# A graph-attention layer on one core: POOL's gathers wait for the landing of the gather five in front, in place of a pace set by its own instructions

## The chip, the cores and the metric

The kernel runs on one core of a Trainium2 chip. The metric is the time of one execution in microseconds (us), measured on the device. PE is the tensor engine, DVE the vector engine, ACT the scalar engine, POOL the GpSimd engine, SP the sync engine, which issues most of the DMAs.

## The reference

The layer takes 12500 nodes of 128 numbers, 412500 edges sorted by their target, and 64 numbers for each edge. With layer norm and ReLU ahead, and the input added at the end, it computes for four heads of 32:

```python
h = (relu(layernorm(x)) @ W_node.T).reshape(12500, 4, 32)
e = (edge_attr_64 @ W_edge.T).reshape(412500, 4, 32)
att = sum(concat([h[src], h[dst], e], -1) * a, -1)
att = where(att > 0, att, 0.2 * att)
m = maximum(segment_max(att, dst), 0.0)
ex = exp(att - m[dst])
denom = segment_sum(ex, dst) + (412500 - deg)[:, None] * exp(-m)
out = x + segment_sum((ex / denom[dst])[:, :, None] * h[src], dst)
```

`h[src]` is the gather: a row of h for each of the 412500 edges.

## The kernel before

Edges are cut into 461 chunks of 896 (7 tiles of 128 edges), and 7 chunks make a batch: 66 batches, the last one with 6 chunks. A batch's rows lie in `hs`, 49 tiles of 128 rows by 144 numbers (h and two attention terms for each head, 576 bytes a row). There are four such buffers in a ring (`RING`), and batch b uses buffer b modulo 4.

Lead-in (lines 241 to 601): the 98 tiles of nodes are normed, multiplied with the weights and written to `table` in DRAM. The first 58 tiles of edges don't wait for the table: POOL gathers their raw rows of x (`gather_raw`, line 256) into the first two buffers, and they go through the same norm and product as the nodes, in groups of up to nine tiles. Raw tiles 0 to 48 are batch 0, raw tiles 49 to 57 are the first nine of batch 1. `lead_in` puts the steps of DVE, ACT and PE in an order that follows from a list of costs. DVE measures each raw tile (line 361) as it lands.

Main loop (from line 1120 on), written out by hand: in iteration b POOL gathers batch b + 1 out of `table`, one indirect DMA for each tile (`gather`, line 707), behind a small memset that waits for PE's last product with the batch that had the buffer. SP loads edge features (`eft`, line 643), the near logits of the targets (`lw`, line 651), `pen` and indices. DVE waits for batch b's rows (`weigh`, through `landed`, line 726), adds up logits (line 808), takes maxima by scans, and multiplies the rows with the weights (line 896); PE sums the rows by target (line 901); DVE adds what is summed to the accumulators (line 995). The last batch is done in two parts: `first_part` takes the tiles with t below `EARLY` (23 gathers), `second_part` the other 15.

How gathers and their readers are tied: each gather of a batch adds 16 to the batch's semaphore when it has landed, one of eight taken in turn by batches (`row_sems`), and the late tiles of the last batch have one of their own; DVE waits for the batch's whole count. The raw gathers have semaphores of the framework, eight in turn, and each waits for the one eight in front. The gathers of line 707 add 1 to `pace` when POOL has finished the instruction, and every second one waits until all but the newest instruction in front of it are finished:

```python
if paced[0] >= BEHIND and paced[0] % STEP == 0:
    nc.gpsimd.wait_ge(pace, paced[0] - BEHIND + 1)
```

Of the kernel before, what the change touches and what calls it, by code (L numbers as in the profile page):

```python
# [20 lines left out]
D = 128  # L21
# [10 lines left out]
CB = 2 * SB - 1  # L32
NBT = -(-NCH // CB)
# [9 lines left out]
EARLY = 4  # L43
# [3 lines left out]
XB = 9  # L47
LOOSE = 1
XS = 3
RAW = (T * CB, XB)  # L50
# [10 lines left out]
ROWSEMS = 8  # L61
# [1 line left out]
LEVELS = 5  # L63
RINGS = 8192
EPS = 1e-5
BEHIND = 2
STEP = 2
WQ = 50
COUNTED = 24
FIRST = 2  # L70
# [57 lines left out]
def kernel(  # L128
# [12 lines left out]
    nc = tc.nc  # L141
# [5 lines left out]
    table = padded[:NB * P, :]  # L147
# [74 lines left out]

    near_sems = [tc.alloc_semaphore(f"near{k}") for k in range(2)]
    near_done = [0, 0]
    late_sems, late_done = [tc.alloc_semaphore("late")], [0]
    pen_sems = [tc.alloc_semaphore(f"pen{k}") for k in range(2)]
    pen_done = [0, 0]
    row_sems = [tc.alloc_semaphore(f"rows{k}") for k in range(ROWSEMS)]
    row_done = [0] * ROWSEMS
    pace, paced = tc.alloc_semaphore("pace"), [0]  # L230

    indices = ctx.enter_context(tc.tile_pool(name="indices", bufs=AHEAD))

# [3 lines left out]
    def index(b):  # L237
        t = indices.tile([P, CB, 2, T], I32, name="ends")
        nc.sync.dma_start(t.rearrange("p q w t -> p (q w t)"), ends[:, chunk_of(b) * 2 * T:(chunk_of(b) + CB) * 2 * T])
        return t  # L240


    with (
        tc.manual_schedule(),
# [6 lines left out]
        early = [index(0)]  # L251
        raw = [pool.tile([P, T * CB, ROW], F32, name="hs") for pool in (opening, second)]

        def gather_raw(k):
            for i in range(RAW[k]):
                nc.gpsimd.indirect_dma_start(
                    out=raw[k][:, i, :D], out_offset=None, in_=x[:, :],
                    in_offset=bass.IndirectOffsetOnAxis(ap=early[k][:, i % CB, 0, i // CB:i // CB + 1], axis=0))

        gather_raw(0)  # L260

        wn = p1.tile([P, D], F32, name="wn")
# [63 lines left out]
        def load_rows(b0, n):  # L326

            s = Rows()
            s.b0, s.n, s.rows = b0, n, None
            at = b0 - NB  # L330
            if at >= 0:
                s.rows = raw[0][:, at:at + n, :] if at < RAW[0] else raw[1][:, at - RAW[0]:at - RAW[0] + n, :]
                s.x = s.rows[:, :, :D]
                return parted(s)
            full = min(n, (N - b0 * P) // P)
            s.x = p3.tile([P, XB, D], F32, name="xg", bufs=5)
            nc.sync.dma_start(s.x[:, :full, :],
                              x[b0 * P:(b0 + full) * P, :].rearrange("(b p) d -> p b d", p=P))
            if full < n:
                nc.vector.memset(s.x[:, full, :], 0.0)  # L340
                rest = N - (b0 + full) * P
                nc.sync.dma_start(s.x[:rest, full, :], x[(b0 + full) * P:N, :])
            return parted(s)

        def parted(s):

            n = s.n
            s.stats = p2.tile([P, XB, 2, 3], F32, name="stats", bufs=5)
            s.units = []
            for i0 in range(0, n, XS):  # L350
                u = Rows()
                u.s, u.i0, u.m = s, i0, min(XS, n - i0)
                u.hn = u.hT = None
                s.units.append(u)
            return s
# [342 lines left out]
    def gather(s, behind=None):  # L698

        if behind is not None:  # L700
            hold = nc.gpsimd.memset(gate, 0.0)
            tc.add_manual_dep(hold.ins, behind.ins.name,
                              mybir.DependencyInfo(mybir.DependencyClass.Sync, mybir.DependencyReason.DATA))
        for t, q in s.tiles:
            if paced[0] >= BEHIND and paced[0] % STEP == 0:
                nc.gpsimd.wait_ge(pace, paced[0] - BEHIND + 1)
            load = nc.gpsimd.indirect_dma_start(  # L707
                out=s.hs[:, t * CB + q, :], out_offset=None, in_=table[:, :],
                in_offset=bass.IndirectOffsetOnAxis(ap=s.ends[:, q, 0, t:t + 1], axis=0),
                engine_sem=pace)  # L710
            paced[0] += 1
            if s.b == NBT - 1 and t >= EARLY:
                by_itself(load, "late", late_sems, late_done, 0)
            else:
                by_itself(load, f"rows{s.b}", row_sems, row_done, s.b % ROWSEMS)

    def by_itself(load, group, sems, done, k):

        load.then_inc(sems[k], 16)
        done[k] += 16  # L720
        tc.add_to_no_dep_group(group, load.ins)
        tc.no_tile_sem_insts.add(load.ins.name)

    def landed(engine, group, sems, done, k, *what):

        wait = engine.wait_ge(sems[k], done[k], synchronizes=[engine.lower_ap(w) for w in what])  # L726
        if what:
            tc.declare_no_dep(wait.ins, group=group, reason="the semaphore counts these loads")
        tc.declare_fence(wait.ins, group=group)
        return wait.ins  # L730

    def load_pen(s):
        s.pen = pen_sb[:, s.b % 2, :]
# [46 lines left out]
    def weigh(s):  # L780

        last = EARLY * CB if s.b == NBT - 1 else T * CB
        s.fence = landed(nc.vector, f"rows{s.b}", row_sems, row_done, s.b % ROWSEMS,
               s.hs[:, RAW[1] if s.b == 1 else 0:last, :],
               *([s.ends[:, :, :, :]] if s.b < NBT - 1 else [])) if s.b else None
        open_weights(s)
        if s.b < NBT - 1:
            landed(nc.vector, f"pen{s.b}", pen_sems, pen_done, s.b % 2, s.pen)
        weigh_part(s, 0, EARLY if s.b == NBT - 1 else T)

    def open_weights(s):
# [45 lines left out]
    def sum_part(s, t0, t1):  # L837

        pa = open_sums()
        got = pa[:, :s.chunks * AW].rearrange("p (q d) -> p d q", d=AW)  # L840
        held = [min(tiles_of(s.c0 + q), t1) for q in range(s.chunks)]
        for q in range(s.chunks):
            if held[q] <= t0:
                nc.vector.memset(got[:, :, q], 0.0)
        for q in range(s.chunks):
            if held[q] > t0:
                multiply(s, q, t0, held[q])
                add_up(s, pa, q, t0, held[q])
        return got
# [11 lines left out]
    def second_part(s):  # L861

        places = columns(s.c0, s.chunks)
        landed(nc.vector, "late", late_sems, late_done, 0, s.hs[:, EARLY * CB:, :], s.ends[:, :, :, :])
        open_weights(s)
        weigh_part(s, *spans[1])
        r = work.tile([P, AW * (MC + 1)], F32, name="r")
        r = r[:, :AW * (len(spans) * s.chunks + 1)].rearrange("p (d c) -> p d c", d=AW)
        nc.scalar.copy(r[:, :, 1::len(spans)], s.first)
        got = sum_part(s, *spans[1])  # L870
        wrap_up(s.b - 1)
        nc.scalar.copy(r[:, :, 2::len(spans)], got)
        return r, s.breaks, places
# [63 lines left out]
    def columns(c, k):  # L937

        _, got = nc.values_load_multi_w_load_instructions(  # L939
            q_rel[0:1, c:c + k], engines=[ENG.DVE], min_val=0, max_val=WQ - 2,  # L940
            skip_runtime_bounds_check_because="near_columns keeps them from 0 to WQ - 2")
        return got
# [129 lines left out]
    def batch(b):  # L1072
        if b not in batches:
            s = batches[b] = Batch()
            s.b = b
            s.hs = None
            s.c0 = chunk_of(b)
            s.chunks = chunk_of(b + 1) - s.c0
        return batches[b]
# [15 lines left out]
    def wrap_up(last):  # L1095

        for b0, n, behind in parts():
            if behind == last:
                at = 4 * b0 - base_of(last)
                stores.append(finish(work, em_ps, b0, n, acc[:, at:at + 4 * n, :]))  # L1100
        if last < NBT - 1 and base_of(last + 1) > base_of(last):
            shift_sums((base_of(last + 1) - base_of(last)) // 4, base_of(last + 1) // 4,
                       nc.gpsimd if last == NBT - 2 else nc.vector)

    with tc.manual_schedule():
# [4 lines left out]
        for k in range(2):  # L1110
            clear_rows(batch(k))
            gather(batch(k))
# [8 lines left out]
        for b in range(NBT - 1):  # L1121
            s = batch(b)
# [11 lines left out]
            if b:  # L1134
                gather(batch(b + 1), scattered.get(b + 1 - RING))
# [46 lines left out]
        s = batch(NBT - 1)  # L1182
# [292 lines left out]
```

## Time and profile before

| | |
|---|---|
| three runs | 4073.79, 4075.94, 4077.2 us |
| profiled execution, its own time | 4069.02 us |
| its span, first to last instruction | 4067.2 us |
| mean granted clock of PE | 0.666 |
| busy: PE, DVE, ACT, POOL | 1392.1, 2428.0, 672.9, 3060.3 us |
| gathers: raw, out of the table | 58, 3165 |
| gathers' queue | 103136 packets, 237.36 MB |

The profile is of one execution. [...] "Idle before" is the time in which the engine did nothing ahead of an instruction, with what ended it. The name `POOL hs L707 <- DMA hs<-table,ends` is a gather that waited, by the trace, for an earlier one. In the timeline the columns are start, duration, engine, line, operation.

### The profile page before, as it was taken

To read this page: it belongs to the slowest core of one execution; us is meant where nothing else is said; L and a number is where in the kernel's file an instruction comes from. 1 tells how busy PE (TensorE), PEld (TensorE's weight loads), DVE (VectorE), ACT (ScalarE), POOL (GpSimd) and SP (SyncE) were. 2 spreads that over 40 slices of the span, in tenths; PEclk is the share of its full clock that TensorE was granted. 3 is DMA by queue.
4 is the path that set the end of the run, shared out by engine and by line. 5 is a ranking of instruction groups with operands and counts; after the bars stand their busy time and mean duration, and the time that the engine had idled before them with its cause. 6 is when DMAs were issued, how large, how long until landed. Compare 5 with 4: busy or idle time off the path is not lost. (4 is left out here: it accounts for less than half of the span.)

```text
span 4067.2 us, 19121 instructions
## 1 busy us (share of the span) xinstructions
PE 1392.1 (34%) x3549; PEld 560.2 (14%) x3549; DVE 2428.0 (60%) x3760; ACT 672.9 (17%) x1688; POOL 3060.3 (75%) x3295
## 2 busy tenths in 40 slices
PE   7453232233332332332332342332331332332331
PEld 5121011011111111110110110110110110110111
DVE  8786555556555567465566465566465465465576
ACT  8121011011011011011011011011011011011121
POOL 7777777777777777777777777777777777777775
PEclk9676666666665676675666665666665666666665
DMA  7543333333333333333333333333333333333332
GB/s 190 166 116 100 109 103 89 106 103 80 112 102 89 107 107 84 102 103 89 107 104 87 103 92 99 107 99 92 103 94 101 103 90 101 102 95 101 107 90 50
DMA packets 243658, 414.96 MB, mean 102 GB/s; under 512 B 71494, under 2 KB 155930, under 8 KB 243532
## 3 DMA queue, kind: packets, MB, share of 16 engines
q0 software_dynamic: 103136, 237.36, 24.4%
q1 hardware_dynamic: 127052, 168.97, 13.2%
q10 hardware_dynamic: 13344, 7.36, 0.6%
q14 instruction: 97, 0.79, 0.1%
q8 instruction: 29, 0.48, 0.1%
HBM read 397.91 MB, written 15.53 MB: 102 GB/s over the span
## 5 line engine op out<-in xcount | busy, mean ns | idle before, releaser
L707 POOL DMA_INDIRECT hs<-table,ends x3165 | 2996.3, 947 | 957.6 <-DMA hs<-table,ends 481.5
L901 PE MATMUL pa<-hs,hot 128*128 128x504 f32 x1820 | 931.6, 677 | 2541.7 <-ACT r L924 2460.7
L808 DVE TENSOR_TENSOR logits<-hs,pick 128x196 f32<-128x196 f32 x65 | 32.4, 499 | 1394.4 <-DVEq L726 1394.2
L901 PEld LDWEIGHTS pa<-hs,hot 128*128 128x128 f32 x1820 | 396.8, 222 | 3068.3 <-ACT r L924 2503.4
L823 ACT ACTIVATE both<-a 32x224 f32<-32x224 f32 (+2 forms) x268 | 103.1, 385 | 2735.8 <-DVE a L821 2733.4
L896 DVE TENSOR_TENSOR hs<-hs,exr 128x1848 f32<-128x1848 f32 (+1 forms) x130 | 451.5, 3515 | 0.0
L757 PE MATMUL z<-eft,wa 128*32 128x512 f32 (+1 forms) x792 | 320.2, 548 | 7.6 <-DMA eft<-in_ef 7.6
L924 ACT COPY r<-pa 32x70 f32<-32x70 f32 (+1 forms) x1040 | 264.4, 254 | 46.6 <-PE pa L901 33.8
L680 DVE COPY_PREDICATED pick<-more,pick 128x1568 f32<-128x1568 int32 (+3 forms) x260 | 253.5, 975 | 8.9
L680 DVE COPY_PREDICATED pick<-more,lw 128x3136 f32<-128x3136 int32 x65 | 240.8, 3705 | 7.3 <-ACT pick L664 1.7
L664 ACT COPY pick<-lw 128x3136 f32<-128x3136 f32 x65 | 182.4, 2806 | 11.2 <-ACTq L726 9.7
L995 DVE TENSOR_TENSOR acc<-acc,up 128x70 f32 x461 | 105.1, 228 | 66.1 <-issue 51.0
L818 DVE TENSOR_TENSOR_SCAN up<-pen_sb,z 32x896 f32<-32x896 f32 (+1 forms) x67 | 133.6, 1994 | 2.3
L820 DVE TENSOR_TENSOR_SCAN m<-pen_sb,up 32x896 f32<-32x896 f32 (+1 forms) x67 | 132.6, 1979 | 2.3
L777 DVE TENSOR_TENSOR hot<-exr,key 128x1568 f32<-128x1568 f32 x65 | 116.4, 1791 | 2.3
L813 DVE TENSOR_TENSOR up<-z,zst 32x224 f32<-32x224 f32 (+2 forms) x268 | 104.3, 389 | 21.2 <-PE z L757 7.5
L757 PEld LDWEIGHTS z<-eft,wa 128*32 128x32 f32 x792 | 79.6, 110 | 244.1 <-issue 235.9
L825 DVE SCALAR_TENSOR_TENSOR both<-pen_sb,up 32x224 f32<-32x224 f32 (+2 forms) x268 | 100.2, 374 | 4.3
L969 ACT ACTIVATE up<-dif 128x14 f32<-128x14 f32 (+2 forms) x35 | 6.5, 185 | 407.5 <-DVE up L967 407.5
L817 DVE TENSOR_TENSOR z<-up,a 32x896 f32<-32x896 f32 (+1 forms) x67 | 72.3, 1080 | 2.3
L821 DVE TENSOR_TENSOR a<-z,m 32x896 f32<-32x896 f32 (+1 forms) x67 | 71.7, 1070 | 2.3
L754 PE MATMUL z<-eft,wa 128*64 128x512 f32 (+1 forms) x132 | 64.6, 571 | 24.0 <-DVE pick L680 24.0
(186 smaller groups left out, 1064.8 us busy)
## 6 DMA issues: line engine op xcount, KB each, us to landing
eft<-in_ef SPq DMA_DIRECT2D x33, 1792.0 KB, 8.1
hs<-table,ends POOLq DMA_INDIRECT x3165
eft<-in_ef SPq DMA_DIRECT2D x33, 1344.0 KB, 6.4
lw<-near SPq DMA_DIRECT2D x461, 64.0 KB
pen_sb<-pens SPq DMA_DIRECT2D x66, 98.1 KB
xg<-in_xh SPq DMA_DIRECT2D x13, 448.0 KB, 5.1
out<-xg SPq DMA_DIRECT2D x13, 448.0 KB, 2.6
table<-rows ACTq DMA_DIRECT2D x8, 648.0 KB, 4.4
```

What stands on the lines that cost most here:

```text
L664: nc.scalar.copy(s.pick[:, :, :s.chunks, :], lw[:, None, :s.chunks, :n].to_broadcast([P, T, s.chunks, n]))
L680: nc.vector.copy_predicated(s.pick[:, :, :s.chunks, :n], bit[:, :, :, None].to_broadcast([P, T, s.chunks, n]), more)
L707: load = nc.gpsimd.indirect_dma_start(out=s.hs[:, t * CB + q, :], out_offset=None, in_=table[:, :], in_offset=bass.IndirectOffsetOnAxis(ap ...
L757: s.made = own_half(s, nc.tensor.matmul(s.z[:, part], wa3[:, j + s.b % 2 * (SB + 1), :], s.eft[:, j, part], start=False, stop=(j == NEXT - ...
L777: nc.vector.tensor_tensor(s.hot.rearrange("p t q r -> p (t q) r"), rows_ps[:, None, :].to_broadcast([P, T * CB, W]), key[:, :, None].to_br ...
L813: on_half(s, nc.vector.tensor_tensor(grouped(up, g), grouped(s.z, g), zst[g * R:(g + 1) * R, t0:t1, :], op=OP.add))
L818: on_half(s, nc.vector.tensor_tensor_scan(up[:, e0:e1], s.pen[:, e0:e1], z, 0.0, op0=OP.add, op1=OP.max))
L820: nc.vector.tensor_tensor_scan(mp[:, ::-1], s.pen[:, e1:e0:-1], up[:, e0:e1][:, ::-1], 0.0, op0=OP.add, op1=OP.max)
L896: nc.vector.tensor_tensor(rows, rows, ex_ps[:, t0:t1, :CB * H, None].to_broadcast([P, t1 - t0, CB * H, HB]), op=OP.mult)
L901: scattered[s.b] = nc.tensor.matmul(wide_ps[:, g, :], s.hot[:, t, g * NEXT:g * NEXT + SB, :].rearrange("p q r -> p (q r)"), flat[:, at:at ...
L924: nc.scalar.copy(r[h * W:(h + 1) * W, q:q + NEXT * len(of) - NEXT + 1:NEXT, :], block)
L995: nc.vector.tensor_tensor(sums, sums, put[:, i0 + i, :, :], op=OP.add)
```

## The change

All gathers, the raw ones too, go through one function, `gather_tile`. Gather n adds 16 on landing to semaphore n modulo 8 of `row_sems`, and before it POOL waits for the landing of gather n - 5 (`OPEN`). The semaphore `pace` and its waits are gone. The gathers that end a group (a batch, up to nine raw tiles, the late tiles) are noted in `closing`; the fifth gather behind such a one adds 1 to a semaphore `ready` when POOL has finished its instruction, and DVE waits for `ready` in place of the landing count (`gathered`). Where the fifth gather behind has not been written yet when DVE's wait is, DVE waits for the last five gathers of the group themselves: so for the last raw group and for the late tiles. DVE now waits for a raw group as a whole, where the rows of the group are first named.

```diff
-BEHIND = 2
-STEP = 2
+OPEN = 5
...
-    late_sems, late_done = [tc.alloc_semaphore("late")], [0]
-    row_done = [0] * ROWSEMS
-    pace, paced = tc.alloc_semaphore("pace"), [0]
+    ready = tc.alloc_semaphore("ready")
+    issued, closing, told = [], {}, {}
...
+    def waits(engine, group, sem, value, *what):
+        wait = engine.wait_ge(sem, value, synchronizes=[engine.lower_ap(w) for w in what])
+        if what:
+            tc.declare_no_dep(wait.ins, group=group, reason="the semaphore counts these loads")
+        tc.declare_fence(wait.ins, group=group)
+        return wait.ins
...
+    def gather_tile(group, rows, of, at):
+        n = len(issued)
+        sem = None
+        if n >= OPEN:
+            nc.gpsimd.wait_ge(*issued[n - OPEN])
+            behind = closing.get(n - OPEN)
+            if behind is not None:
+                sem = ready
+                told[behind] = len(told) + 1
+        load = nc.gpsimd.indirect_dma_start(
+            out=rows, out_offset=None, in_=of[:, :], in_offset=bass.IndirectOffsetOnAxis(ap=at, axis=0),
+            engine_sem=sem)
+        apart(load, group, row_sems[n % ROWSEMS])
+        issued.append((row_sems[n % ROWSEMS], 16 * (n // ROWSEMS + 1)))
+        for k in [k for k, v in closing.items() if v == group]:
+            del closing[k]
+        closing[n] = group
+
+    def gathered(group, *what):
+        if group in told:
+            return waits(nc.vector, group, ready, told[group], *what)
+        n = next(k for k, v in closing.items() if v == group)
+        for i in range(n - OPEN + 1, n):
+            nc.vector.wait_ge(*issued[i])
+        return waits(nc.vector, group, *issued[n], *what)
...
             for i in range(RAW[k]):
-                nc.gpsimd.indirect_dma_start(
-                    out=raw[k][:, i, :D], out_offset=None, in_=x[:, :],
-                    in_offset=bass.IndirectOffsetOnAxis(ap=early[k][:, i % CB, 0, i // CB:i // CB + 1], axis=0))
+                gather_tile(f"raw{k}{i // XB}", raw[k][:, i, :D], x, early[k][:, i % CB, 0, i // CB:i // CB + 1])
...
             if at >= 0:
-                s.rows = raw[0][:, at:at + n, :] if at < RAW[0] else raw[1][:, at - RAW[0]:at - RAW[0] + n, :]
+                k, i = (0, at) if at < RAW[0] else (1, at - RAW[0])
+                s.rows = raw[k][:, i:i + n, :]
+                gathered(f"raw{k}{i // XB}", s.rows, *([early[k][:, :, :, :]] if i + n == RAW[k] else []))
...
         for t, q in s.tiles:
-            if paced[0] >= BEHIND and paced[0] % STEP == 0:
-                nc.gpsimd.wait_ge(pace, paced[0] - BEHIND + 1)
-            load = nc.gpsimd.indirect_dma_start(
-                out=s.hs[:, t * CB + q, :], out_offset=None, in_=table[:, :],
-                in_offset=bass.IndirectOffsetOnAxis(ap=s.ends[:, q, 0, t:t + 1], axis=0),
-                engine_sem=pace)
-            paced[0] += 1
-            if s.b == NBT - 1 and t >= EARLY:
-                by_itself(load, "late", late_sems, late_done, 0)
-            else:
-                by_itself(load, f"rows{s.b}", row_sems, row_done, s.b % ROWSEMS)
+            late = s.b == NBT - 1 and t >= EARLY
+            gather_tile("late" if late else f"rows{s.b}", s.hs[:, t * CB + q, :], table, s.ends[:, q, 0, t:t + 1])
...
-        s.fence = landed(nc.vector, f"rows{s.b}", row_sems, row_done, s.b % ROWSEMS,
+        s.fence = gathered(f"rows{s.b}",
                s.hs[:, RAW[1] if s.b == 1 else 0:last, :],
...
-        landed(nc.vector, "late", late_sems, late_done, 0, s.hs[:, EARLY * CB:, :], s.ends[:, :, :, :])
+        gathered("late", s.hs[:, EARLY * CB:, :], s.ends[:, :, :, :])
```

The lines of the gathers become 274 (before: 256 and 707), that of DVE's wait 254 (before: 726), that of the logits 833 (before: 808). On PE, ACT and SP the order of the work stays as it was.

The order of POOL's instructions where the raw gathers end and those of the table begin, before. The names in brackets are the semaphores that POOL waits for: DMASW are the framework's eight for raw gathers, DMAHW tell that the table is written.

```order
L256 DMA hs<-in_x,ends 128x128 [waits DMASW7_49]
L256 DMA hs<-in_x,ends 128x128 [waits DMASW0_49]
L256 DMA hs<-in_x,ends 128x128 [waits DMASW1_49]
L707 DMA hs<-table,ends 128x144 [waits DMAHW4_49,DMAHW5_49,DMAHW3_49,DMAHW6_49,DMAHW2_49,DMAHW7_49,DMAHW1_49,DMAHW0_49]
L707 DMA hs<-table,ends 128x144
L707 DMA hs<-table,ends 128x144 [waits pace]
```

The same place after the change (rows0 to rows7 are `row_sems`):

```order
L274 DMA hs<-in_x,ends 128x128 [waits rows2]
L274 DMA hs<-in_x,ends 128x128 [waits rows3]
L274 DMA hs<-in_x,ends 128x128 [waits rows4]
L274 DMA hs<-table,ends 128x144 [waits DMAHW3_49,DMAHW4_49,DMAHW2_49,DMAHW5_49,DMAHW1_49,DMAHW6_49,DMAHW0_49,DMAHW7_49,rows5,DVE_sequencer_49]
L274 DMA hs<-table,ends 128x144 [waits rows6]
L274 DMA hs<-table,ends 128x144 [waits rows7]
```

Each gather now has a wait, and the first one out of the table has one more, DVE_sequencer: it waits until DVE has passed its own wait for the last raw group. That wait stands on DVE ahead of the statistics of raw tiles 36 to 41, after the change:

```order
L429 RECIPROCAL rstd<-rstd 128x9 [waits Activation_49]
L431 SCALAR_TENSOR_TENSOR shift<-tot,rstd 128x9 [waits DVE_49]
L472 MEMSET hs 128x12x2 [waits Activation_49]
L446 TENSOR_SCALAR hn<-hs,rstd,shift 128x128
L410 BN_STATS stats<-hs 128x6 [waits rows7,rows6,rows0,rows5,rows1,DMAHW0_49,DVE_sequencer_49]
L410 BN_STATS stats<-hs 128x6 x5
```

Before, DVE had no wait for a group there: each of the statistics waited for the landing of its own tile (DMASW). On DVE at the beginning of the first part of the last batch, before:

```order
L854 MEMSET pen_sb 32x1 [waits pen1,DVE_sequencer_49]
L856 MEMSET breaks 128x12
L857 COPY breaks<-new 128x6 [waits DVE_49]
L808 TENSOR_TENSOR logits<-hs 128x4x24 [waits DVE_49,rows1,PE_49,DVE_sequencer_49]
L810 STREAM_TRANSPOSE zst<-logits 128x128 [waits DVE_49]
```

and after:

```order
L879 MEMSET pen_sb 32x1 [waits pen1,DVE_sequencer_49]
L881 MEMSET breaks 128x12
L882 COPY breaks<-new 128x6 [waits DVE_49]
L833 TENSOR_TENSOR logits<-hs 128x4x24 [waits DVE_49,ready,PE_49,DVE_sequencer_49]
L835 STREAM_TRANSPOSE zst<-logits 128x128 [waits DVE_49]
```

The wait for the landing count of the 23 gathers (rows1) has become one for `ready`, which POOL raises at the end of the fifth of the late gathers behind them.

More of the change, by code (lines that the diff above doesn't have):

```diff
@@ L240, in index, with apart, by_itself, landed @@
         return t
+    def apart(load, group, sem):
+        load.then_inc(sem, 16)
+        tc.add_to_no_dep_group(group, load.ins)
+        tc.no_tile_sem_insts.add(load.ins.name)
+    def by_itself(load, group, sems, done, k):
+        apart(load, group, sems[k])
+        done[k] += 16
+    def waits(engine, group, sem, value, *what):
[4 more added lines that the diff above has]
+        return wait.ins
+    def landed(engine, group, sems, done, k, *what):
+        return waits(engine, group, sems[k], done[k], *what)
+    def gather_tile(group, rows, of, at):
[22 more added lines that the diff above has]
+        return waits(nc.vector, group, *issued[n], *what)
     with (
@@ L704, in gather @@
         for t, q in s.tiles:
-            if paced[0] >= BEHIND and paced[0] % STEP == 0:
-                nc.gpsimd.wait_ge(pace, paced[0] - BEHIND + 1)
-            load = nc.gpsimd.indirect_dma_start(
-                out=s.hs[:, t * CB + q, :], out_offset=None, in_=table[:, :],
-                in_offset=bass.IndirectOffsetOnAxis(ap=s.ends[:, q, 0, t:t + 1], axis=0),
-                engine_sem=pace)
-            paced[0] += 1
-            if s.b == NBT - 1 and t >= EARLY:
-                by_itself(load, "late", late_sems, late_done, 0)
-            else:
-                by_itself(load, f"rows{s.b}", row_sems, row_done, s.b % ROWSEMS)
[L717 to L730, printed above, removed]
+            late = s.b == NBT - 1 and t >= EARLY
+            gather_tile("late" if late else f"rows{s.b}", s.hs[:, t * CB + q, :], table, s.ends[:, q, 0, t:t + 1])
     def load_pen(s):
```

## The prediction

> **What bounds the kernel now.** I read the page's busy times first, then the groups of line 707, then the timeline of POOL alone, then the waits, and last the chain that ended last.
>
> ```profile
> PE 1392.1 (34%) x3549; PEld 560.2 (14%) x3549; DVE 2428.0 (60%) x3760; ACT 672.9 (17%) x1688; POOL 3060.3 (75%) x3295
> L707 POOL DMA_INDIRECT hs<-table,ends x3165 | 2996.3, 947 | 957.6 <-DMA hs<-table,ends 481.5
> L707 POOL DMA_INDIRECT hs<-table,ends x3165: 940/944/1833, 75.7 to 4035.3; - x198
> 4012.82 0.94 POOL L707 DMA_INDIRECT hs<-table,ends  x1 [0.30 <-DMA hs<-table,ends]
> 4014.07 0.94 POOL L707 DMA_INDIRECT hs<-table,ends  x1 [0.30 <-issue]
> 4015.31 0.94 POOL L707 DMA_INDIRECT hs<-table,ends  x1 [0.30 <-DMA hs<-table,ends]
> DVE logits L808 <- DVEq L726: 1404.7, 64, 30.8
> ```
>
> No engine is above 75% busy, yet POOL never rests. Line 707 is busy for 2996.3 us and idle before its instructions for 957.6 us, 3953.9 us together, and its starts run from 75.7 to 4035.3, which is 3959.6 us. So a gather costs POOL about 1.249 us: 0.944 busy and a fixed 0.30 between two. The timeline has that 0.30 both before a gather that waits for the semaphore `pace` and before its neighbour that waits for nothing ("issue"), so the waits of today cost nothing. DVE waits 1404.7 us in 64 batches, some 22 us in each, for gathers to land. The kernel is POOL's chain of 3165 gathers out of the table, with 58 raw ones before it, and a tail of 32 us behind the last one. Whatever delays one gather delays the end, since POOL has no slack in which to catch up.
>
> **The new wait in the long middle.** A gather may now start when the one five in front has landed. Left alone it starts 5 x 1.249 = 6.24 us after that one. So the wait is free while a landing, and POOL's waking on it, take less than 6.24 us from the start of the instruction.
>
> ```profile
> L256 POOL DMA_INDIRECT hs<-in_x,ends x58: 940/944/1110, 3.1 to 74.4; - x58
>   issue: 17.1, 56
> DMA to landing us min/median/max: 2.5/4.4/5.5
> 4016.56 2.56 DMA hs<-table,ends
> 4019.30 0.33 DVE L808 TENSOR_TENSOR logits<-hs 128x96 f32<-128x96 f32 x1 [8.59 <-DVEq L726]
> ```
>
> The third row is of the 58 raw gathers (line 256), which run while the loads of x fill the DMA engines: 4.4 us in the median, 5.5 at most. They too wait for a landing, eight in front, and 17.1 us over 56 is the same 0.30 us, so a wait for a landing costs nothing by itself. The fourth row, of the chain, is a gather with quiet DMA engines: 2.56 us, and DVE starts 0.18 us later, 2.74 us after the gather's start. In quiet stretches the wait has 3.5 us to spare.
>
> The loud stretches are the loads of eft, two sizes of 33 each.
>
> ```profile
> eft<-in_ef SPq DMA_DIRECT2D x33, 1792.0 KB, 8.1
> eft<-in_ef SPq DMA_DIRECT2D x33, 1344.0 KB, 6.4
> 2010.00:2012.00 2.00, 0.00 (x0) 0.00 (x0) 0.00 (x0) 0.00 (x0) 1.39 (x3) 0.50 1.04 423
> 3599.64 0.39 SPq L643 DMA_DIRECT2D eft<-in_ef  x1
> 3599.66 0.94 POOL L707 DMA_INDIRECT hs<-table,ends  x1 [0.30 <-DMA hs<-table,ends]
> q0 software_dynamic: 103136, 237.36, 24.4%
> q0 software_dynamic: 32, 0.07, 6.9%
> q0 software_dynamic: 56, 0.15, 9.3%
> q0 software_dynamic: 64, 0.15, 8.9%
> ```
>
> The window row (last two columns: share of the DMA engines, GB/s) shows them full during such a load. The last four rows count the packets of the gathers' queue: in the whole span, and from 3599.64 to 3604.2, to 3605.0 and to 3605.3. A gather has 32 packets (103136 over 3165 + 58). Up to 3604.2 there are only the 32 of the gather before. Those of the gather that starts at 3599.66, together with the load, begin behind 3604.2 and are complete by 3605.3: its data is 4.5 to 5.6 us behind its start. The same count for the quiet gather of 4016.56 gives:
>
> ```profile
> q0 software_dynamic: 59, 0.15, 28.4%
> q0 software_dynamic: 64, 0.15, 27.2%
> ```
>
> to 4018.7 and to 4018.8, so 2.24 us, and its consumer starts 0.50 us behind that. For the gather beside the load this makes 5.64 + 0.50 = 6.14 us if its completion is no slower than in quiet, just inside 6.24. If the completion is stretched as the data is (5.64 / 2.24 = 2.5 times 0.50) it is 6.9, which is 0.65 us too late. So a load of eft costs 0 to 0.65 us, once: the gathers behind the first delayed one land with it in a bunch, and POOL's pause gives them time. I take 0.25, the lower half, since the raw gathers of a busier stretch have a maximum of 5.5. With 66 loads that is 66 x 0.25 = 16.5 us, bounds 0 and 42.9.
>
> [...]
>
> **From the raw gathers to the table.** The first gather out of the table is now also behind DVE's wait for the last raw group, since it writes the same buffer. DVE comes to that wait in front of the statistics of raw tile 36.
>
> ```profile
> 69.41 0.94 POOL L256 DMA_INDIRECT hs<-in_x,ends  x1 [0.30 <-issue]
> 71.88 0.67 DVE L361 BATCH_NORM_STATS2 stats<-hs 128x6 f32<-128x128 f32 x3
> 74.42 0.94 POOL L256 DMA_INDIRECT hs<-in_x,ends  x1 [0.30 <-DMA table<-rows]
> 75.67 0.94 POOL L707 DMA_INDIRECT hs<-table,ends  x1 [0.30 <-issue]
> 79.09 0.32 DVE L397 TENSOR_SCALAR hn<-hs,rstd,shift 128x128 f32<-128x128 f32 x1
> 79.32 1.25 DVE L361 BATCH_NORM_STATS2 stats<-hs 128x6 f32<-128x128 f32 x6
> ```
>
> The six statistics at 79.32 are tiles 36 to 41, counted back from the last of the 58. The last raw gather starts at 74.42 and lands by 77.0 (2.56), so it is not what DVE waits for. But DVE is at the wait only when line 397 is issued at 79.09, and POOL stands until then: 79.09 plus about 0.3 to wake, 79.4, in place of 75.67. That is 3.7 us, all on POOL's chain. Lower bound 1.7, if DVE's sequencer comes to the wait as soon as the raw gather has landed (77.0 + 0.4 - 75.67). Upper bound 4.5, if DVE is late itself. DVE is not held up there, and if a raw gather stalls before it, that vanishes in this wait. DVE's earlier waits of the lead-in I cost at nothing: the last of them asks for the end of raw gather 53, which starts at 69.41 and is done at 70.35, and DVE comes to it at 71.88.
>
> **The tail.** DVE learns that a batch has landed when POOL has finished the instruction of the fifth gather behind it. In the middle this is about 4.7 us later than today and eats into 22 us of waiting; the loads that SP issues behind DVE's wait move along with it, and the gathers they serve are a batch or more ahead. At the end nothing covers it.
>
> ```profile
> 4022.81 0.94 POOL L707 DMA_INDIRECT hs<-table,ends  x1 [0.30 <-DMA hs<-table,ends]
> 4035.29 0.94 POOL L707 DMA_INDIRECT hs<-table,ends  x1 [0.30 <-DMA hs<-table,ends]
> 4036.61 1.80 DVE L995 TENSOR_TENSOR acc<-acc,up 128x70 f32 x7
> 4038.41 1.18 DVEq L939
> 4040.30 0.28 DVE L808 TENSOR_TENSOR logits<-hs 128x72 f32<-128x72 f32 x1 [1.88 <-DVEq L726]
> L726 DVEq EVENT_SEMAPHORE  x204: 21/50/50, 154.0 to 4039.8; - x102
> ```
>
> The chain that ended last leaves POOL at 4016.56, with the last gather of the first part, not with the last gather of all. From 4019.30 DVE works without a break that a gather causes: to 4038.41, then 1.18 us of register loads, then the second part at 4040.30. The last gather starts at 4035.29 and has landed by 4037.9. The fifth gather behind 4016.56 is that of 4022.81; it ends at 4023.75, and DVE can start at 4023.75 + 0.18 = 4023.93 instead of 4019.30: 4.6 us later. All that follows on DVE moves by it. The four further waits of the second part are for gathers that landed long before, and run while DVE has nothing to do: 0 (bound 0.2, four times the 50 ns of the last row).
>
> **The sum.** 16.5 + 3.7 + 4.6 = 24.8 us. What is removed, the `pace` increment and its wait, saves nothing, since raw gathers without either have the same period. The profiled execution took 4069.02 us (span 4067.2, 1.8 around it), so it would take 4093.8. The three runs of before have a median of 4075.94, 6.9 us above that execution; I carry the difference along: 4100.7, forecast 4101.
>
> **Rivals.** One: the window is never too short, by 6.14 against 6.24, or because DMA engines serve the gathers' queue in between after all. For it speaks the raw maximum of 5.5; against it that 0.1 us is all there is to spare beside a load. Then only 3.7 + 4.6 = 8.3 us are left, and if DVE's sequencer runs ahead of its engine 1.7 + 4.6 = 6.3: 4082 to 4084, at the border of what a measurement here can tell from no change (0.2%, 8.2 us). This is the not-slower side; it decides at a landing, with waking, of 6.24 us.
>
> Two: a gather beside a load lands whole only when its slowest DMA engine is done, and that engine is far behind the others. The price is a landing as late as the load's own, 8.1 us by its row, so up to 8.1 + 0.2 - 6.24 = 2 us; at half of it, 1 us, it is 66 us for all loads and 74 with the rest: 4150. For it: all sixteen parts must be in. Against it: the count is complete at 3605.3, 2.4 us before the load's end.
>
> Three: the excess of line 707, 3165 x 0.944 = 2987.8 against 2996.3 busy, is time lost to too many gathers in flight, and goes. That gains 8.5 us and, beside rival one, cancels the rest: 4075. Against it: with landings of 2.56 us only two or three are in flight, fewer than the five that the change allows.
>
> **Chances and range.** Forecast, stalls of 0.1 to 0.65 us a load: 0.72. Rival one 0.15, rival two 0.1, rival three 0.03. The range reaches from 4075.94 + 8.3 (no stall beside loads, 4084) to 4075.94 + 8.3 + 42.9 = 4127. Faster by over 0.2%: 0.02; within 0.2%: 0.12, most of rivals one and three; slower: 0.86.
>
> **What would show it.** In the profile of the changed kernel: line 274's gathers 1.249 us apart except for one pause of 0.1 to 0.6 us in each batch, about 6 us behind a load of eft, summing to some 16 us of idle time before POOL that a DMA ended; the first table gather 3.7 us behind its grid; DVE's wait ahead of the first part of the last batch ended by POOL some 7.4 us after the last gather of that part started. Wrong would be: no pauses beside the loads, pauses of over 0.65 us, a fixed interval other than 1.249, or DVE becoming late for POOL at the gates.

## The result and the profile after

| | before | after |
|---|---|---|
| median of 6 runs each | 4075.54 us (4073.79 to 4077.2) | 4092.36 us (4091.46 to 4096.22) |
| profiled execution | 4069.02 us, span 4067.2 | 4092.19 us, span 4090.4 |
| ratio after / before, 95% interval | | 1.0044 [1.0031, 1.0057] |

The change makes the kernel 16.8 us slower by the medians and 23.2 us by the two profiled executions. The profile of before is of an execution 6.5 us under its median, that of after lies on its median. What follows takes the 23.2 us apart, since only these two executions have traces; the 6.4 us by which it exceeds the 16.8 may be a difference between executions of before, and nothing tells in which stretch it would lie.

The page of after, with POOL's busy time, the shares of the chain that ended last, and the group of the table gathers (line 274 now):

```profile
PE 1375.8 (34%) x3549; PEld 554.3 (14%) x3549; DVE 2440.8 (60%) x3760; ACT 672.9 (16%) x1688; POOL 3060.2 (75%) x3295
POOL 66%; issue 22%; DMA 11%; DVE 1%; ACT 0%; POOLq 0%; DVEq 0%; ACTq 0%
L274 POOL DMA_INDIRECT hs<-table,ends x3165 | 2996.0, 947 | 974.6 <-issue 923.8
```

POOL's chain of gathers is still the kernel. Its busy time is the same to 0.3 us; its idle time has grown from 957.6 to 974.6 us. The view of line 274 tells where its gathers begin and end, and what its idle times (us, times) ended with:

```profile
L274 POOL DMA_INDIRECT hs<-table,ends x3165: 938/944/1832, 80.1 to 4053.6; - x198
  DMA hs<-table,ends: 47.2, 113
  DMA hs<-in_x,ends: 3.5, 7
  DVEq L254: 3.3, 1
```

The first row splits the time into three, and the same row of every later run does so too. **Up to the first table gather**: 80.1 us, before 75.7, so 4.4 more. **From the first to the last**: 3973.5 us, before 3959.6, so 13.9 more. **From the start of the last gather to the end**: 4090.4 - 4053.6 = 36.8 us, before 31.9, so 4.9 more. Together 23.2.

The timeline at the first table gather, POOL and DVE:

```profile
75.94 0.94 POOL L274 DMA_INDIRECT hs<-in_x,ends  x1 [0.30 <-issue]
80.15 0.94 POOL L274 DMA_INDIRECT hs<-table,ends  x1 [3.26 <-DVEq L254]
79.65 0.32 DVE L446 TENSOR_SCALAR hn<-hs,rstd,shift 128x128 f32<-128x128 f32 x1
79.96 1.26 DVE L410 BATCH_NORM_STATS2 stats<-hs 128x6 f32<-128x128 f32 x6
```

POOL starts 0.19 us behind DVE's statistics of tiles 36 to 41 and stood 3.26 us, 2.96 more than its fixed 0.30. The rest of the 4.4 is 1.5 us by which the raw gathers already ran late: seven of them paused for a landing, 3.5 us in place of 7 x 0.30.

In the middle, the waits of POOL from 200 to 4030 us (us in total, times, longest):

```profile
POOL hs L274 <- issue: 892.1, 2946, 1.4
POOL hs L274 <- DMA hs<-table,ends: 43.0, 109, 1.4
```

109 gathers waited for a landing, 43.0 us in place of 109 x 0.30. One of them, POOL, SyncE's load and the view of that stretch's DMAs:

```profile
2637.90 0.94 POOL L274 DMA_INDIRECT hs<-table,ends  x1 [0.30 <-issue]
2642.89 0.94 POOL L274 DMA_INDIRECT hs<-table,ends  x1 [0.30 <-issue]
2644.65 0.94 POOL L274 DMA_INDIRECT hs<-table,ends  x1 [0.81 <-DMA hs<-table,ends]
2638.04 0.41 SPq L692 DMA_DIRECT2D eft<-in_ef  x1
eft<-in_ef SPq DMA_DIRECT2D x1, 1792.0 KB
```

The gather at 2637.90, 0.14 us ahead of the load's issue, is the fifth in front of the one at 2644.65. With POOL's waking it took 6.75 us to land, 0.51 more than the window of 6.24. Counted over the whole trace (each load of eft, and what POOL stood beyond its fixed 0.30 us, in idle times of over 0.33 us, for a gather issued beside the load), 25 of the 33 loads of 1792 KB are followed by such a pause, 7.5 us in sum, and 7 of the 33 of 1344 KB, 3.1 us. Of these 32 pauses 30 are of 0.04 to 0.59 us; two are longer, 1.08 and 1.14:

```profile
207.10 0.94 POOL L274 DMA_INDIRECT hs<-table,ends  x1 [1.38 <-issue]
3944.96 0.94 POOL L274 DMA_INDIRECT hs<-table,ends  x1 [1.44 <-DMA hs<-table,ends]
```

The other 3.3 us of the 13.9 are nearly all in two pauses beside other loads. The longer one is in the lead-in:

```profile
115.00 0.94 POOL L274 DMA_INDIRECT hs<-table,ends  x1 [2.71 <-DMA hs<-table,ends]
```

The gather five in front of it started at 106.36, while SyncE issued four loads of `in_dstc` (from 105.14 on). The other one is 0.70 us at 1287.11, behind a gather of 1280.04 beside a load of `in_xh` (1280.09). No run leaves these loads out.

The tail: POOL and the chain that ended last, then DVE and ACT.

```profile
4034.84 0.94 POOL L274 DMA_INDIRECT hs<-table,ends  x1 [0.30 <-issue]
4041.08 0.95 DMA hs<-table,ends
4042.22 0.32 DVE L833 TENSOR_TENSOR logits<-hs 128x96 f32<-128x96 f32 x1 [8.59 <-DVEq L254]
4042.86 4.31 ACT L949 COPY r<-pa 32x35 f32<-32x35 f32 x16 [17.52 <-PE pa L926]
4048.93 1.26 ACT L848 ACTIVATE both<-a 32x128 f32<-32x128 f32 x4 [1.76 <-DVE a L846]
```

The last gather of the first part starts at 4034.84, the fifth behind it at 4041.08, and DVE 0.19 us after that one's end: 7.38 us after the last gather, 2.74 before. The two ACT rows matter further down.

### The profile page after: what moved, and what is told of

It reads as the page before. It is cut to its first block, busy times and chain, and to the rows that moved or that the text cites. A ratio compares the mean times of both kernels' runs of the same rounds, so it can differ in the third digit from the quotient of the medians.

```text
span 4090.4 us, 19124 instructions
## 1 busy us (share of the span) xinstructions
PE 1375.8 (34%) x3549; PEld 554.3 (14%) x3549; DVE 2440.8 (60%) x3760; ACT 672.9 (16%) x1688; POOL 3060.2 (75%) x3295
## 4 chain that ended last, share of the span: by engine, by line
POOL 66%; issue 22%; DMA 11%; DVE 1%; ACT 0%; POOLq 0%; DVEq 0%; ACTq 0%
POOL hs L274 66%; DMA hs<-table,ends 11%; DMA hs<-in_x,ends 0%; POOL gate L750 0%; DVE hs L903 0%; DVE stats L410 0%; DVE acc L1020 0%; ACT both L848 0%; DVE up L838 0%; DVE up L1013 0%; DVE up L843 0%; DVE m L845 0%; DMA ends<-in_ends 0%; POOLq L274 0%; DVE up L1004 0%
## 5 line engine op out<-in xcount | busy, mean ns | idle before, releaser
L274 POOL DMA_INDIRECT hs<-table,ends x3165 | 2996.0, 947 | 974.6 <-issue 923.8
L926 PE MATMUL pa<-hs,hot 128*128 128x504 f32 x1820 | 914.7, 666 | 2581.9 <-ACT r L949 2498.9
L802 DVE TENSOR_TENSOR hot<-exr,key 128x1568 f32<-128x1568 f32 x65 | 116.4, 1792 | 2.3
```

Of the source, the lines that this page charges most:

```text
L274: load = nc.gpsimd.indirect_dma_start(out=rows, out_offset=None, in_=of[:, :], in_offset=bass.IndirectOffsetOnAxis(ap=at, axis=0), engine_ ...
L802: nc.vector.tensor_tensor(s.hot.rearrange("p t q r -> p (t q) r"), rows_ps[:, None, :].to_broadcast([P, T * CB, W]), key[:, :, None].to_br ...
L926: scattered[s.b] = nc.tensor.matmul(wide_ps[:, g, :], s.hot[:, t, g * NEXT:g * NEXT + SB, :].rearrange("p q r -> p (q r)"), flat[:, at:at ...
```

## The experiments

Twelve kernels ran, four at a time, each four on one chip and beside the kernel before. The second four are told first: on their chip the kernel before took 4068.74 us (4066.7 to 4071.57, 19 runs), and POOL bounds what is traced there (with eight open none of its idle times from 200 to 4030 us is longer than 0.3 us). The changed kernel itself was not among those four, so they are split by the same three stretches.

| run | median, us | ratio to before, 95% | first table gather | first to last | last to end |
|---|---|---|---|---|---|
| after (its own comparison) | 4092.36 | 1.0044 [1.0031, 1.0057] | +4.4 | +13.9 | +4.9 |
| two waits out, 5 open | 4083.96 | 1.0037 [1.0023, 1.0050] | +0.6 | +9.1 | +4.0 |
| two waits out, 8 open | 4079.36 | 1.0024 [1.0015, 1.0033] | +1.2 | +0.5 | +7.0 |
| no loads of eft | 4080.40 | 1.0027 [1.0017, 1.0038] | +3.4 | +3.3 | +4.8 |
| 4 open | 4181.22 | 1.0275 [1.0259, 1.0291] | +8.3 | +99.2 | +3.4 |

The last three columns are us against the profiled execution of before, from the spans 4080.9, 4075.9, 4078.7 and 4178.1 and these rows of line 274, in the order of the table:

```profile
L274 POOL DMA_INDIRECT hs<-table,ends x3165: 938/944/1705, 76.3 to 4045.0; - x198
```
```profile
L274 POOL DMA_INDIRECT hs<-table,ends x3165: 940/944/1827, 76.9 to 4037.0; - x198
```
```profile
L274 POOL DMA_INDIRECT hs<-table,ends x3165: 938/944/1703, 79.1 to 4042.0; - x198
```
```profile
L274 POOL DMA_INDIRECT hs<-table,ends x3165: 938/944/1567, 84.0 to 4142.8; - x198
```

**The two single waits out, five open.**

```diff
-        if group in told:
+        if group in told and group != f"rows{NBT - 1}":
...
-                gathered(f"raw{k}{i // XB}", s.rows, *([early[k][:, :, :, :]] if i + n == RAW[k] else []))
+                gathered(f"raw{k}{i // XB}", s.rows, *([early[k][:, :, :, :]] if k == 0 and i + n == RAW[k] else []))
```

> The changed kernel with its two single waits taken out: the batch at the end waits for its own last five landings and not for POOL's word, and DVE's wait on the last raw group no longer names the indices, so the first gather out of the table is not behind it. The window of five stays. Theory (the changed kernel's 16.8 us are landing pauses beside loads of eft plus these two waits): 4.9 us of the tail and 3 to 4.5 us at the first table gather go, 7.9 us less than the changed kernel, so 4084 to 4085 where the kernel before takes 4075.5 (ratio 1.0022); in the profile the first table gather has 0.30 us of idle time in front, DVE's first part of the last batch starts 2.7 us after its last gather, and some 14 us of idle time ended by landings are still in front of the table gathers. Rival (the window costs nothing, the two waits are all): within 1 us of the kernel before.

The timeline at the two places that the edits touch, POOL's first table gather and DVE's first part of the last batch:

```profile
76.33 0.94 POOL L274 DMA_INDIRECT hs<-table,ends  x1 [0.30 <-issue]
4029.11 0.32 DVE L833 TENSOR_TENSOR logits<-hs 128x96 f32<-128x96 f32 x1 [4.01 <-DVEq L254]
```

Both waits are gone: the gather has its fixed 0.30 in front, and DVE starts 15.9 us ahead of the last gather, as before the change (16.0). Yet the tail is only 0.9 us shorter than after, where the theory had 4.9. By the two ratios the time is some 3 us below that of after, not 7.9. By the two profiled spans it is 9.5 us below, but 4.8 of these lie in the middle, 9.1 us in place of 13.9 under the same window of five: 35 loads of eft have a pause, 8.5 us in sum where the 32 of after have 10.6, and the pauses in the lead-in are shorter. Why is open. That the time is the expected 4084 us is luck: the kernel before takes 4068.74 us here and not 4075.5, and the ratio is 1.0037 where 1.0022 was expected. The rival, that the window costs nothing, is out: the time is 15.2 us over before. Further rows of that tail, PE, ACT and DVE:

```profile
4005.13 0.50 DVE L833 TENSOR_TENSOR logits<-hs,pick 128x196 f32<-128x196 f32 x1 [6.53 <-DVEq L254]
4020.10 14.92 PE L926 MATMUL pa<-hs,hot 128*128 128x504 f32 x28 [38.70 <-DVE hs L921]
4035.06 4.31 ACT L949 COPY r<-pa 32x35 f32<-32x35 f32 x16 [18.25 <-PE pa L926]
4039.39 1.27 ACT L848 ACTIVATE both<-a 32x128 f32<-32x128 f32 x4
4040.69 0.69 DVE L856 STREAM_TRANSPOSE exr<-both 128x128 f32<-128x128 f32 x2 [3.78 <-ACT both L848]
```

The second-last batch is also told of late (its logits at 4005.13). Its matmuls and then ACT's copies of their sums (line 949) move with it, the last batch's exponentials (line 848) stand behind those copies on ACT, and DVE waits 3.78 us for them. Before the change the same place of ACT's timeline has 2.32 us to spare:

```profile
4019.38 4.31 ACT L924 COPY r<-pa 32x35 f32<-32x35 f32 x16 [16.96 <-PE pa L901]
4026.02 1.26 ACT L823 ACTIVATE both<-a 32x128 f32<-32x128 f32 x4 [2.32 <-DVE a L821]
```

So the late word costs the tail twice in parallel: on DVE for the last batch (4.6 us) and through PE and ACT for the one before it. Taking the last batch's away leaves the other; the reverse was not run.

**The same with eight open** (`OPEN = 8`): a window of 9.99 us.

> As the run with the two waits taken out, and with eight gathers allowed to be open in place of five, so that a gather may wait up to 9.99 us for the landing. Theory: landings beside a load of eft take 5.6 to 6.6 us, so no gather out of the table waits for one; idle time in front of the table gathers beyond 0.30 us each falls from some 14 us to under 1 us, and the time is the kernel before's, within 3 us. Rival (a per-gather cost of the wait on the landing's semaphore, or of eight semaphores in turn): as slow as with five open, 8 us over the kernel before.

The waits from 200 to 4030 us:

```profile
POOL hs L274 <- issue: 915.3, 3025, 0.3
POOL hs L274 <- DMA hs<-table,ends: 11.3, 37, 0.3
```

No idle time is longer than the fixed 0.3: the pauses are gone, and the middle stretch is within 0.5 us of before. So the wait, the eight semaphores and the landing counts cost nothing by themselves; only the width of the window does. The time, though, is 10.6 us over before, not within 3. It lies in the tail. POOL's word now comes three gathers later, 3.75 us, for the second-last batch too:

```profile
4000.85 0.50 DVE L833 TENSOR_TENSOR logits<-hs,pick 128x196 f32<-128x196 f32 x1 [6.89 <-DVEq L254]
4035.77 0.69 DVE L856 STREAM_TRANSPOSE exr<-both 128x128 f32<-128x128 f32 x2 [6.76 <-ACT both L848]
```

The logits start 36.2 us ahead of the last gather, with five open 39.9. DVE's wait for ACT is 6.76 in place of 3.78 us, 2.98 more, and the tail is 3.0 longer. That the tail moves with this wait shows the path through the second-last batch. The rival's number, 8 us over before, was met in size, but not by its mechanism. The first table gather stands 1.2 us longer, since the last write of the table, which it needs, is issued at 73.17 here and at 70.40 before, and the semaphore of that write is the last of those that it waits for, at 75.85:

```profile
73.17 0.37 ACTq L475 DMA_DIRECT2D table<-rows  x1
76.89 0.94 POOL L274 DMA_INDIRECT hs<-table,ends  x1 [1.51 <-issue]
```

Why ACT comes to it later is open.

**No loads of eft** from batch 2 on: the edge features are a constant and do not enter the result.

```diff
-        nc.sync.dma_start(s.eft[:, :n, :], ef[k0:k0 + n * P, :].rearrange("(j p) e -> p j e", p=P))
+        if s.b < 2:
+            nc.sync.dma_start(s.eft[:, :n, :], ef[k0:k0 + n * P, :].rearrange("(j p) e -> p j e", p=P))
+        else:
+            nc.scalar.copy(s.eft[:, :n, :].rearrange("p j e -> p (j e)"), eps.to_broadcast([P, n * CE]))
```

> The changed kernel, but from batch 2 on the tile eft is filled by ScalarE with a constant and its load is left out, so the edge features do not enter the result. Theory (the pauses in the steady stretch come from the loads of eft): the 33 pauses of 0.1 to 1.1 us there, 9.8 us in sum, go; the idle time in front of the table gathers behind 200 us falls to under 2 us beyond the fixed 0.30 each, and the time falls by some 10 us, to about 4082, if ScalarE's fill is hidden. Rival (the pauses come from the loads of indices, the writes of the output or the gathers among themselves): pauses of the same size stay, and the time stays at 4092.

The waits from 200 to 4030 us:

```profile
POOL hs L274 <- issue: 907.1, 2999, 0.3
POOL hs L274 <- DMA hs<-table,ends: 19.4, 63, 0.4
```

The longest idle time is 0.4 us, where the changed kernel has 1.4: without the loads of eft the pauses of the steady stretch do not occur, as the theory has it, and the rival (indices, outputs, the gathers themselves) is out: what is left there is under 0.2 us. The rest of the middle, 3.3 us, lies ahead of 200 us, most of it in front of one gather of the lead-in, as the same view from 76.5 to 200 us has it:

```profile
POOL hs L274 <- DMA hs<-table,ends: 5.4, 6, 3.0
```

The other two stretches keep their wait and their tail.

**Four open** (`OPEN = 4`): a window of 4.99 us.

> The changed kernel with four gathers open in place of five: a gather may wait 4.99 us for the landing in place of 6.24. Theory (a gather issued together with a load of eft lands, with POOL's waking, 5.6 to 6.6 us after its start): every load of eft now costs a pause, 0.6 to 1.6 us each, 1.1 in the mean, 66 x 1.1 = 73 us in place of some 14, less 1.2 us in the tail: 4145 to 4155. Rival (only every second load comes beside a gather whose landing is late): half of that, some 36 us, 4115. Rival (landings have a short tail just past 6.24 us and few lie between 4.99 and 6.24): 66 x 0.25, about 4095.

99 us more in the middle, beyond the theory's 73 and far from both rivals. Counted as above, every one of the 66 loads is now followed by pauses, 45.8 us behind those of 1792 KB and 39.4 us behind those of 1344 KB, 1.39 and 1.19 us each. Since POOL now waits at every load, the trace has the landings: from the start of the late gather to that of the one that waited for it, the first at each load, it is 6.32 us in the median beside the larger loads and 6.12 beside the smaller, and over 6.24 us at 20 and 12 of the 33. It fits that, with five open, the larger loads mostly cost something and the smaller mostly nothing. Another 18 us are pauses away from the loads of eft, some of them in the lead-in, which the theory did not have; what causes them is open. POOL's busy time in the table gathers is 4.1 us shorter (2992.2 us), so that the middle grows by 99 us in all.

**Two other chips.** The eight remaining kernels ran on two chips on which the kernel before takes 4758.27 (35 runs) and 4758.82 us (31 runs). There POOL is not the bound (in six of the eight its last gather starts 134 to 162 us ahead of the end, in the kernels above 32 to 39), so their totals say nothing on the terms above; their expectations were sized for the kernel at 4075 us. The first four: the last batch waiting for its own landings (the first edit above alone), the last raw group's wait without the indices (the second edit alone), both, and both with eight open.

> Against the changed kernel, the first part of the last batch waits for the landings of its own last five gathers in place of ready; all else stays. Theory (the excess is three parts: DVE's late notice at the end 4.9 us, DVE's wait in front of the first table gather 3.0, pauses at landings 15): 4.6 to 5 us faster than the changed kernel, and in the profile DVE's logits of the first part 2.7 us after the start of its last gather, not 7.4. Rival (the end hangs on the last gather, the late notice is covered by the 1.88 us ahead of the second part and by what follows): within 1 us of the changed kernel.

> Against the changed kernel, DVE's wait for the last raw group no longer names the indices of batch 1, so that the first table gather does not wait for DVE. Theory: that gather starts 1.25 us after the one in front (3.26 us of idle before, 0.3 now), and as POOL has no slack the end comes 3 us earlier. Rival (a lead-in delay is made up, because the pauses behind it fall to other places relative to the loads of that stretch): under 1 us of gain.

> Against the changed kernel, the two edits of the first two runs together; what is left of the change is the wait for the landing five in front alone. Theory: 7.9 us faster than the changed kernel, so some 9 to 15 us slower than before, all of it as idle time of POOL between two gathers that a landing ended. Rival (the pauses are no more than what POOL's long instructions of before were): within 3 us of before.

> As the run before, with the landing eight in front (a window of 9.98 us in place of 6.24). Theory: no landing takes that long, so POOL's idle time of over 0.33 us between two gathers goes from some 15 us to under 1, and the time is that of before within 3 us. Rival (waiting for landings costs POOL something by itself, whatever the distance): as slow as the run with five in front.

Then both edits with the second-last batch also waiting for its own landings, with five, six and eight open, and the changed kernel unaltered:

```diff
-        if group in told:
+        if group in told and group not in (f"rows{NBT - 2}", f"rows{NBT - 1}"):
```

> The changed kernel with three single waits taken out: the last two batches (not the last alone) wait for their own five landings and not for POOL's word, and DVE's wait on the last raw group no longer names the indices. The window of five stays. Theory (in the earlier run the second-last batch, told late, held ScalarE's copies and so the last batch's exponentials 3.8 us, as much as the last batch's own word had cost): from the start of the last gather to the end it takes 32.0 us as in the kernel before, in place of 35.9; what is left over the kernel before is the landing pauses, 10 to 14 us. Rival (the tail is long for another reason): 35 us or more from the last gather to the end, and 14 to 18 us over the kernel before.

> As the run before it, with six gathers open, so that a gather may wait 7.49 us for the landing. Theory (landings beside a load of eft take 5.6 to 6.6 us, with the wake 5.9 to 6.9): none or nearly none of the pauses is left, under 2 us in sum, and the time is the kernel before's within 3 us. Rival (landings have a long tail, as the 1.6 us a load at four open suggests): 3 us or more of pauses are left.

> As the run before it, with eight gathers open, 9.99 us. Theory: no pause, 32.0 us from the last gather to the end, the kernel before's time plus 1 to 2 us (the first gather out of the table came 1.2 us late in the earlier run with eight). Rival (eight semaphores or the longer wait behind eight landings cost something on every gather or batch): 5 us or more over the kernel before, as the tail of the earlier run with eight was 7 us longer.

> The changed kernel itself, unaltered, so that the three others are compared with it on one chip. Expected from its first runs: 16.8 us over the kernel before (ratio 1.004), and, in its profile, some 14 us of idle time ended by landings in front of the table gathers, 2.95 us in front of the first of them, 36.8 us from the last gather to the end.

| run | median, us | ratio to before, 95% |
|---|---|---|
| last batch alone | 4748.06 | 0.9983 [0.9974, 0.9992] |
| raw wait alone | 4746.48 | 0.9983 [0.9975, 0.9992] |
| both, 5 open | 4747.19 | 0.9984 [0.9975, 0.9994] |
| both, 8 open | 4756.13 | 0.9995 [0.9986, 1.0004] |
| last two batches, 5 open | 4747.00 | 0.9972 [0.9961, 0.9983] |
| last two batches, 6 open | 4757.32 | 0.9995 [0.9986, 1.0003] |
| last two batches, 8 open | 4757.69 | 0.9998 [0.9990, 1.0007] |
| after, unaltered | 4749.35 | 0.9986 [0.9973, 1.0000] |

In the last of these (after, unaltered; span 4759.1) the waits show POOL at its gates, and ACT ahead of its copies, held by something that the profile names only as remote; the row below them is line 274's:

```profile
POOL gate L750 <- remote: 430.2, 27, 21.9
ACT r L949 <- remote: 1198.4, 41, 64.9
L274 POOL DMA_INDIRECT hs<-table,ends x3165: 938/944/1813, 142.6 to 4607.1; - x198
```

Its last gather starts at 4607.1, 152 us ahead of the end. A longer wait of POOL vanishes in these, and the changed kernel is no slower there than the kernel before. What holds the other engines up on these chips is open. Whether the tail returns to 32 us when both batches wait for their own landings, the question of the fifth kernel here, could therefore not be seen.

One thing can be read in spite of it, POOL's idle time for landings at the table gathers. With five open (after; then the last two batches on their own landings), six and eight:

```profile
  DMA hs<-table,ends: 25.6, 44
```
```profile
  DMA hs<-table,ends: 21.4, 40
```
```profile
  DMA hs<-table,ends: 9.0, 26
```
```profile
  DMA hs<-table,ends: 8.5, 28
```

Less 0.30 each time that is 12.4, 9.4, 1.2 and 0.1 us. The view puts other idle times of over 0.33 us down to "issue", 70 and 91 with five open, 34 and 31 with six and eight, so that five may cost more here than these rows say. Still, one more gather in the window takes nearly all of the pauses away, as expected for six open (under 2).

## Why the prediction was right, step by step

- **What bounds the kernel**: right. POOL's interval stayed at 1.249 us, and each pause of POOL shows in the end.
- **The window beside the loads, 16.5 us**: the mechanism held, and the runs show it: in the middle eight open cost 0.5 us and four 99.2, without the loads the pauses of the steady stretch are gone (under 0.2 us left), and on another chip six open leave 1.2 us of POOL's idle time for landings in place of 9.4. The size was off, and in two ways that partly cancel. The loads of eft cost 10.6 us, 0.16 a load and not 0.25, since 34 of the 66 cost nothing. The 3.3 us of pauses beside other loads had no term. The 0.25 was picked between 0 and 0.65, so that the sum of the middle came near is in part luck: another kernel with five open has 0.13 a load and 9.1 us in all. A pause of over 0.65 us was named as a sign of being wrong, and two loads have one (1.08 and 1.14). They lie above the bound that the stretched completion gave, and what makes them so long is open.
- **Why a gather beside a load lands late**: open. In the kernel before, the loads' queue moved 296 packets of some 3.6 KB from 3599.64 to 3604.2 us (`q1 hardware_dynamic: 296, 1.06, 74.1%`), 18.5 for each of the 16 DMA engines, while the gather of 3599.66 had not moved one. In what order the engines take packets from two queues no run shows; the 16.5 us rest on the times of the packets and of the landings alone.
- **The first table gather, 3.7 us**: 2.96 us of waiting and 1.5 us of late raw gathers, 4.4 together, at the upper bound of 4.5. The releaser is the predicted one (DVE's sequencer), in front of the predicted statistics. A raw gather's pause was said to vanish in this wait. It did so in part: the last raw gather starts 1.5 us later than before, and DVE, which ends the wait, begins those statistics 0.64 us later (79.96, before 79.32). With four open the last raw gather starts 4.9 us later and the statistics 4.5 us later (83.81), so late raw gathers move DVE too.
- **The tail, 4.6 us**: 4.9. The time of the word, 7.38 us after the last gather, is as forecast. What was missed is the second-last batch: its late word was put down as covered by DVE's 22 us of waiting, but the cover there is ACT's 2.32 us. It cost nothing extra only because the last batch's own delay ran beside it.
- **The sum**: 24.8 us against 23.2 between the two profiled executions. The step that failed is the last, the 6.9 us between before's profiled execution and its median, carried along to 4100.7. The profiled execution of after lies 0.2 us from its median. By the medians the change costs 16.8 us, a third less than the 24.8 of the sum. On the chip of the second four the kernel before takes 4068.74 us, as in its profiled execution. Where the execution at 4075 spends its 6.5 us more has no trace.
- **Rivals**: one (no pause) and two (1 us a load) are out by the 13.9 us. Three, that the excess of long gathers goes with fewer in flight, is out: busy 2996.0 after, 2996.3 before.

## What to carry to other kernels

A bound on transfers in flight is free as long as the slowest landing fits into the window, so size it by landings beside the largest load and not by quiet ones: between the first and the last table gather four open cost 99 us here, five 9 to 14, eight under 1, and six some 1 us by POOL's idle time on another chip. A word that one engine passes on at the end of a later instruction is late by that many instructions (here 7.38 us after the last gather in place of 2.74). That cost the tail 4.9 us here; in the middle, where DVE waits some 22 us a batch, nothing of it shows (0.5 us in all with eight open). So look where the pipeline drains, at every batch still in it and at each engine's own spare time, since taking away one late word can leave another just as long.

## What was not expected of the hardware

The same kernel before took 4068.74, 4075.54, 4758.27 and 4758.82 us in the comparisons of this study, and on one of the two chips at 4758 us the unaltered change cost nothing (0.9986 [0.9973, 1.0000]). The 0.4% was measured where POOL is the bound, and it holds for no more than that.
